# One operand turned on TensorE instead of through memory, in the tail of a two-layer graph network

## The chip, the core and the metric

The kernel runs on one core of a Trainium2 chip. The metric is the device time of one execution, in microseconds (us); lower is better. The core has TensorE (PE) for matrix products, VectorE (DVE), ScalarE (ACT) and GpSimd (POOL) for the rest, and SyncE (SP), which here only issues DMAs. Each engine takes its own instructions in order.

## What is computed

128 graphs go through the same two layers, each with 128 nodes of 512 features (`x`, float32) and a 128x128 adjacency matrix (`adj`). Cut to what matters:

```python
# layer 0
h = relu(layernorm(x))
r = relu(hypergraph_conv(h, adj, W1, b1))        # 512 -> 1024 features
y = hypergraph_conv(layernorm(r), adj, W2, b2)   # 1024 -> 512 features
x = x + (y + h)
# layer 1
h = relu(layernorm(x))
agg = (adj @ h) / max(rowsum(adj), 1e-6)
x = x + relu(concat([h, agg]) @ W.T)             # W: 512 x 1024
# hypergraph_conv(h): D^-1 H B^-1 H^T (h @ W.T) + b, with H = (adj != 0)
```

## The kernel before, in words

The work of one graph is cut into some fifty small stages, each a function with the graph's number as its argument. Each stage issues its instructions at once, in the order in which the stages are called; there is no scheduler that moves them. The function `step(s)` calls the stages of several graphs in turn, so that while one graph is in its first weighted product another is in its last one. `head()` starts this pipeline up, and `tail()` runs it dry for the last five graphs, called a, b, c, d and e (e is graph 127). The order of every engine's instructions is therefore the order of these calls, written out by hand.

A weighted product (`product`, L387) keeps near-float32 precision with three parts of each operand: a high part (`h`), a low part (`l`) and a part for the difference (`d`). The bank whose name ends in `m` (`rm`, `gm`, `bm`, `am`) takes the products of high and low parts (L401), the bank ending in `d` (`rd`, `gd`, `bd`, `ad`) the third (L406). ScalarE then copies the main bank out and VectorE adds the difference bank. The names are: `r` for the first convolution, `g` for the second, `b` for layer 1's neighbour half ("mean"), and `a` for its own half ("self"), on which `aggregate` (L616) adds the mean's part through the adjacency (`anp`). `py` (L534) is the second convolution's product with the node matrix. The high part comes from ScalarE (L483), the low one from a subtraction on GpSimd or VectorE (`combine`, L80; GpSimd in pieces of 256 columns), the third from VectorE (L492).

TensorE contracts over the partitions, so an operand that lies with nodes on partitions has to be turned before a weighted product. Before the change every graph does it by a round trip: `trip_out` (L447) writes the tile to memory, four DMAs of `trip_in` (L455) read it back as 32x32 blocks in swapped places, and VectorE turns each block in place (L462). For layer 1 the stages are `layer1_norm` (L256: ScalarE, relu of the normalised `x_t`), `layer1_trip_out` (`h_scratch`), `layer1_trip_in` (`hb`), `layer1_turn` (`ht`), `layer1_high` (`hh`), `layer1_low` (`hl`) and `layer1_rest` (`hd`). The 1024-wide operand `n` and the adjacency (`an_scratch`, `anb`, L214) make such trips too. The read-back tile leaves its features in an order that goes with blocks of 32, and the weights are loaded in the same order.

`hb` of one graph and `gb_t`, the mean's result, share one buffer (tag "hbt"), so a graph's trip in waits until the graph before it has split its mean. Six banks of PSUM are handed round for products, two for small ones.

`fill(n)` (L94) issues matmuls of a constant over n columns into the next bank that is handed out, ahead of that bank's own product. They compute nothing that is used. They stand where TensorE would otherwise wait.

The order of the tail on TensorE is: `py` of c, first convolution of e, `b` and `a` of b, `g` of d, aggregate of b, filler, `py` of d, `b` and `a` of c, `g` of e, aggregate of c, filler, `py` of e, `b` and `a` of d, aggregate of d, filler, `b` and `a` of e, aggregate of e.

Of the kernel before, what the change touches and what calls it, by code (L numbers as in the profile page):

```python
# [7 lines left out]
FP = mybir.dt.float32  # L8
FR = mybir.dt.float32r
# [15 lines left out]
def gnn_kernel(  # L25
# [31 lines left out]
    nc = tc.nc  # L57
# [51 lines left out]
    def stage(f):  # L109

        def run(g, *a):
            key = f, g, *(v for v in a if type(v) is int)
            if 0 <= g < N and key not in done:
                done.add(key)
                f(g, *a)

        return run


# [104 lines left out]
    @stage  # L224
    def load_adj(g):
        ADJ[g] = pool.tile([P, P], FP, tag="adj", name="adj_t")
        nc.sync.dma_start(out=ADJ[g], in_=adj[g])
# [20 lines left out]
    @stage  # L248
    def scales(g, kind):
        t = STATS[kind, g]  # L250
        nc.vector.reciprocal(t[:, 4:5], t[:, 3:4])
        nc.vector.tensor_tensor(t[:, 5:6], t[:, 1:2], t[:, 4:5], MUL)  # L252
# [8 lines left out]
    @stage  # L261
    def mean_operator(g):

        a = ADJ.pop(g)
        deg = pool.tile([P, 1], FP, tag="deg", name="deg", bufs=2)
        nc.vector.tensor_reduce(deg, a, AX.X, ADD)
        nc.vector.tensor_scalar(deg, deg, EPS_DEG, 1.0 / 4096.0, MAX, MUL)
        nc.vector.reciprocal(deg, deg)
        nc.vector.tensor_scalar(a, a, deg, None, MUL)
        ADJ[g] = a  # L270

    @stage
    def mean_out(g):
        ANT[g] = trip_out(ADJ.pop(g), "an")

    @stage
    def mean_in(g):
        d = ANT[g]
        ANT[g] = pool.tile([P, P], FP, tag="anb", name="anb")
        load_blocks(ANT[g], d)  # L280
# [17 lines left out]
    @stage  # L298
    def mean_rest(g):
        SPLIT.pop(("an", g))()  # L300
# [112 lines left out]
    @stage  # L413
    def conv1_weights(g, half):
        PR[g, half] = product(Z[g], w1[half : half + 1], lambda pm: PY.update({(g, half): pm}), "r")

    @stage
    def conv1_main(g, half):
        if half == 0:
            R[g] = pool.tile([P, DH], FP, tag="r", name="r")  # L420
        copy(R[g][:, HALVES[half]], PY.pop((g, half)), AF.Copy, scale=DN[g][:, 1:2])  # L421

    @stage
    def conv1_out(g, half):
        r, dn = R[g][:, HALVES[half]], DN[g]
        nc.vector.scalar_tensor_tensor(r, PR.pop((g, half)), dn[:, 0:1], r, MUL, ADD)  # L426

    @stage
    def conv1_bias(g, half, eng=nc.gpsimd):
        r = R[g][:, HALVES[half]]  # L430
        combine(eng, r, r, b1_bc[:, HALVES[half]], ADD)
# [5 lines left out]
    @stage  # L437
    def inner_spread(g):
        spread((2, g), R[g], pool.tile([P, DH], mybir.dt.bfloat16, tag="junk", name="junk"), DH)
# [26 lines left out]
    @stage  # L466
    def inner_out(g):
        NT[g] = trip_out(R.pop(g), "n")

    @stage  # L470
    def inner_in(g):
        NT[g] = trip_in(NT[g], "t2", "n")
# [24 lines left out]
    @stage  # L497
    def inner_turn(g):
        NT[g] = turned(NT[g], "t1", "n")

    @stage
    def inner_high(g):
        NT[g] = split_high(("n", g), NT[g], ("t3", "t2", "t1"))

    @stage
    def inner_low(g, *eng):
        NT[g][0](*eng)

    @stage
    def inner_rest(g):  # L510
        N_LEFT[g] = NT.pop(g)[1]()


    @stage
# [12 lines left out]
    @stage  # L527
    def conv2_bias(g, eng=nc.gpsimd):
        combine(eng, G[g], G[g], c0, ADD)

    @stage
    def conv2_nodes(g):
        PY[g] = py = small_bank("py")
        nc.tensor.matmul(py, S.pop(g), G.pop(g), start=True, stop=True)  # L534
# [11 lines left out]
    @stage  # L546
    def layer1_spread(g):
        spread((3, g), X[g], H3[g], D)

    @stage  # L550
    def layer1_norm(g):
        normalise((3, g), H3[g], X[g], AF.Relu)

    @stage
    def layer1_trip_out(g):
        H3T[g] = trip_out(H3.pop(g), "h")
# [9 lines left out]
    @stage  # L566
    def layer1_high(g):
        H3T[g] = split_high(("h", g), H3T[g], ("h2", "h3", "h1"))

    @stage  # L570
    def layer1_low(g, *eng):
        H3T[g][0](*eng)

    @stage
    def layer1_rest(g):
        H_LEFT[g] = H3T.pop(g)[1]()

    @stage
    def layer1_mean(g):
        PB[g] = product(H_LEFT[g], w3[:1], lambda pm: PY.update({("b", g): pm}), "b")  # L580
# [14 lines left out]
    @stage  # L595
    def layer1_mean_low(g, *eng):
        GB[g][0](*eng)
# [21 lines left out]
    @stage  # L619
    def layer1_self_out(g):  # L620
        o, pd = OP[g]
        nc.vector.scalar_tensor_tensor(o, pd, 4096.0, o, MUL, ADD)
# [301 lines left out]
    def tail():  # L924
        a, b, c, d, e = range(N - 5, N)
        layer1_self_main(a)
        conv2_bias(c)
        layer1_high(b)
        conv2_nodes(c)
        layer1_self_out(a)  # L930
        mean_out(b)
        inner_out(d)
        inner_in(d)
        finish(a)
        layer1_low(b)
        load_adj(c)
        mean_in(b)
        conv1_main(e, 0)
        conv2_out(c)
        conv1_weights(e, 1)  # L940
        layer1_sums(c)
        layer1_spread(c)
        layer1_rest(b)
        conv1_out(e, 0)
        conv1_main(e, 1)
        layer1_mean(b)
        inner_turn(d)
        scales(c, 3)
        layer1_self(b)
        conv1_out(e, 1)  # L950
        inner_high(d)
        conv1_bias(e, 0)
        layer1_norm(c)
        layer1_mean_main(b)
        mean_transpose(b)
        conv1_bias(e, 1)
        inner_low(d)
        layer1_mean_out(b)
        layer1_trip_out(c)
        inner_sums(e)  # L960
        layer1_mean_high(b)
        inner_spread(e)
        scales(e, 2)
        inner_rest(d)
        layer1_mean_low(b)
        conv2_weights(d)
        mean_operator(c)
        mean_rest(b)
        layer1_mean_rest(b)
        aggregate(b)  # L970
        inner_norm(e)
        conv2_main(d)
        layer1_trip_in(c)
        conv2_weights_out(d)
        layer1_turn(c)
        layer1_self_main(b)
        conv2_bias(d)
        layer1_high(c)
        fill(384)
        conv2_nodes(d)  # L980
        layer1_self_out(b)
        mean_out(c)
        inner_out(e)
        load_adj(d)
        inner_in(e)
        finish(b)
        layer1_low(c)
        mean_in(c)
        conv2_out(d)
        layer1_sums(d)  # L990
        layer1_rest(c)
        layer1_spread(d)
        layer1_mean(c)
        inner_turn(e)
        scales(d, 3)
        layer1_self(c)
        inner_high(e)
        layer1_norm(d)
        layer1_mean_main(c)
        mean_transpose(c)  # L1000
        layer1_mean_out(c)
        inner_low(e)
        layer1_trip_out(d)
        layer1_mean_high(c)
        mean_operator(d)
        inner_rest(e)
        layer1_mean_low(c, nc.vector)
        conv2_weights(e)
        mean_rest(c)
        layer1_mean_rest(c)  # L1010
        aggregate(c)
        conv2_main(e)
        layer1_trip_in(d)
        conv2_weights_out(e)
        layer1_turn(d)
        layer1_self_main(c)
        conv2_bias(e)
        layer1_high(d)
        fill(768)
        conv2_nodes(e)  # L1020
        layer1_self_out(c)
        layer1_low(d)
        mean_out(d)
        finish(c)
        mean_in(d)
        conv2_out(e)
        load_adj(e)
        layer1_sums(e)
        layer1_rest(d)
        layer1_mean(d)  # L1030
        layer1_spread(e)
        scales(e, 3)
        layer1_self(d)
        layer1_norm(e)
        layer1_mean_main(d)
        mean_transpose(d)
        layer1_mean_out(d)
        layer1_trip_out(e)
        layer1_mean_high(d)
        mean_operator(e)  # L1040
        layer1_mean_low(d, nc.vector)
        mean_rest(d)
        layer1_mean_rest(d)
        aggregate(d)
        layer1_trip_in(e)
        layer1_turn(e)
        layer1_self_main(d)
        layer1_high(e)
        layer1_self_out(d)
        mean_out(e)  # L1050
        layer1_low(e, nc.vector)
        mean_in(e)
        layer1_rest(e)
        fill(1536)
        layer1_mean(e)
        finish(d)
        layer1_self(e)
        layer1_mean_main(e)
        mean_transpose(e)
        layer1_mean_out(e)  # L1060
        layer1_mean_high(e)
        mean_rest(e)
        layer1_mean_low(e)
        layer1_mean_rest(e)
        aggregate(e)
        layer1_self_main(e)
        layer1_self_out(e)
        finish(e)
# [40 lines left out]
```

## Time and profile before

| | us |
|---|---|
| median of 4 runs | 2503.28 |
| lowest and highest run | 2502.23 to 2504.00 |
| the profiled execution | 2503.60 |
| its span, first to last instruction | 2501.8 |
| TensorE busy | 2475.6 (99%) |
| VectorE, ScalarE, GpSimd busy | 1999.5, 1935.0, 1713.2 |
| span from 2441 on, roughly the tail | 61 |
| first matmul of e's product `bm` | 2489.50 |
| TensorE's last matmul ends | 2497.20 |

The profile is of one execution. Its times are counted from the first instruction. A timeline line gives start, duration, engine, source line, operation, output and inputs, and in brackets the idle time before it with what ended it. The chain of waits is followed back from the last instruction. A window line gives the busy time of the engines in a stretch in the order TensorE, its weight loads, VectorE, ScalarE, GpSimd, then the granted clock of TensorE, the DMA share and GB/s. Neighbouring instructions of one engine overlap a little, so that a VectorE operation of 0.69 us is followed by the next one 0.61 us after its start. The profiled execution spends 1.8 us outside its span.

### The profile page before, as it was taken

The numbers are of one execution on the slowest core, as the hardware profiler recorded it, in microseconds if no ns is written. First come the engines' busy times: TensorE is split into PE (matmuls) and PEld (weight loads), VectorE is DVE, ScalarE is ACT, GpSimd is POOL, SyncE is SP. The second block draws the span as 40 slices with busy tenths as digits, with TensorE's granted clock in tenths as the row PEclk, the third lists the DMA queues.
The fourth block names the chain that finished last, engine by engine and source line by source line (L and its number), as shares of the span: only waits on it lengthen the run. The fifth ranks groups of instructions, "written<-read, shape, count | busy, mean of one in ns | idle before, by whom it ended". The sixth has DMA issues, their size and how long they took to land.

```text
span 2501.8 us, 41081 instructions
## 1 busy us (share of the span) xinstructions
PE 2475.6 (99%) x11196; PEld 2004.0 (80%) x11196; DVE 1999.5 (80%) x4910; ACT 1935.0 (77%) x4112; POOL 1713.2 (68%) x2284
## 2 busy tenths in 40 slices
PE   8899999999999999999999999999999999999998
PEld 5688888888888888888888888888888888888886
DVE  7888887887888788888878888887887888788785
ACT  6788778778877877887787788778778877877874
POOL 2476677677667767766776776677677667767763
PEclk9999999999999999999999999999999999999999
DMA  6333443443344344334434433443443344344332
GB/s 176 108 120 119 131 126 120 128 131 120 118 126 132 120 128 131 120 119 131 127 120 128 131 120 118 131 128 120 128 129 122 119 132 126 120 128 130 120 113 94
DMA packets 409671, 311.87 MB, mean 125 GB/s; under 512 B 176736, under 2 KB 340576, under 8 KB 409440
## 3 DMA queue, kind: packets, MB, share of 16 engines
q1 hardware_dynamic: 408608, 309.18, 40.0%
q8 instruction: 88, 1.44, 0.3%
q14 instruction: 143, 1.17, 0.2%
q10 hardware_dynamic: 576, 0.07, 0.0%
q0 software_dynamic: 256, 0.01, 0.0%
HBM read 166.47 MB, written 142.61 MB: 124 GB/s over the span
## 4 chain that ended last, share of the span: by engine, by line
PE 95%; DVE 2%; DMA 1%; ACT 1%; SPq 1%; issue 0%; POOL 0%; POOLq 0%; DVEq 0%; ACTq 0%
PE rm L401 18%; PE gm L401 18%; PE gd L406 9%; PE bm L401 9%; PE am L401 9%; PE rd L406 9%; PE bd L406 5%; PE ad L406 4%; PE pz L359 4%; PE py L534 4%; PE am L616 2%; PE ad L616 1%; PE ps_s L321 1%; DMA w11r<-in_w1t_dram 0%; DMA nb<-n_scratch 0%
## 5 line engine op out<-in xcount | busy, mean ns | idle before, releaser
L80 POOL TENSOR_TENSOR g<-g,c 128x256 f32<-128x256 f32 x252 | 180.9, 739 | 648.2 <-DVE g L525 648.2
L80 POOL TENSOR_TENSOR r<-r,b_bc 128x256 f32<-128x256 f32 x500 | 359.7, 741 | 54.1 <-DVE r L426 44.5
L80 POOL TENSOR_TENSOR nl<-nt,nh 128x256 fp32r<-128x256 f32 x504 | 357.5, 737 | 4.2 <-ACT nh L483 4.2
L80 POOL TENSOR_TENSOR x_t<-x_t,b_bc 128x256 f32<-128x256 f32 x256 | 242.2, 965 | 15.2 <-DMA b_bc<-in_b_dram 15.2
L240 ACT ACTIVATE h<-x_t 128x512 f32<-128x512 f32 x256 | 160.0, 625 | 106.3 <-DVE x_t L538 104.0
L610 ACT ACTIVATE o<-am 128x512 f32<-128x512 f32 x128 | 76.6, 598 | 214.1 <-PE am L616 214.1
L80 POOL TENSOR_TENSOR hl<-ht,hh 128x256 fp32r<-128x256 f32 x252 | 235.3, 953 | 2.5 <-ACT hh L483 2.3
L80 POOL TENSOR_TENSOR x_t<-x_t,h 128x256 f32<-128x256 f32 x256 | 180.8, 725 | 42.1 <-ACT h L256 42.1
L256 ACT ACTIVATE h<-x_t,st 128x512 f32<-128x512 f32 x256 | 206.1, 805 | 1.9 <-DVE st L252 1.8
L426 DVE SCALAR_TENSOR_TENSOR r<-rd,dinv,r 128x512 f32<-128x512 f32 x256 | 190.6, 745 | 19.1 <-PE rd L406 18.4
L589 DVE TENSOR_TENSOR gb_t<-bd,gb_t 128x512 f32<-128x512 f32 x128 | 88.6, 692 | 141.8 <-ACT gb_t L585 139.4
L538 DVE SCALAR_TENSOR_TENSOR x_t<-py,dinv,x_t 128x512 f32<-128x512 f32 x128 | 96.1, 751 | 123.7 <-PE py L534 123.6
L80 POOL TENSOR_TENSOR bl<-gb_t,bh 128x256 fp32r<-128x256 f32 x252 | 180.5, 735 | 15.5 <-PE am L401 15.5
L245 ACT ACTIVATE h<-x_t,st 128x512 f32<-128x512 f32 x256 | 183.9, 718 | 4.3
L359 PEld LDWEIGHTS pz<-s,h 128*128 128x128 f32 x1024 | 133.5, 191 | 66.3 <-ACT s L323 46.4
L421 ACT ACTIVATE r<-rm,dinv 128x512 f32<-128x512 f32 x256 | 172.9, 676 | 1.7 <-PE rm L401 1.7
L525 DVE TENSOR_TENSOR g<-gd,g 128x512 f32<-128x512 f32 x128 | 88.5, 692 | 97.7 <-PE gd L406 92.4
L462 DVE STREAM_TRANSPOSE nt<-nb 128x1024 f32<-128x1024 f32 x128 | 157.4, 1230 | 2.0 <-DMA nb<-n_scratch 1.6
L256 ACT ACTIVATE r<-r,st 128x1024 f32<-128x1024 f32 x128 | 157.7, 1232 | 1.3 <-DVE st L252 1.3
L492 DVE SCALAR_TENSOR_TENSOR nd<-nh,nl 128x1024 fp32r<-128x1024 f32 x128 | 155.8, 1217 | 0.0
L627 DVE SCALAR_TENSOR_TENSOR o<-o,x_t 128x512 f32<-128x512 f32 x128 | 151.0, 1180 | 4.3
L401 PE MATMUL rm<-w11h,z 128*128 128x512 f32 x512 | 151.4, 417 | 0.0
(138 smaller groups left out, 7207.2 us busy)
## 6 DMA issues: line engine op xcount, KB each, us to landing
n_scratch<-r SPq DMA_DIRECT2D x128, 512.0 KB, 2.7
nb<-n_scratch SPq DMA_DIRECT2D x512, 128.0 KB, 2.8
x_t<-in_x_dram SPq DMA_DIRECT2D x128, 256.0 KB, 3.0
h_scratch<-h SPq DMA_DIRECT2D x128, 256.0 KB, 2.0
hb<-h_scratch SPq DMA_DIRECT2D x512, 64.0 KB, 2.0
out_dram<-o SPq DMA_DIRECT2D x128, 256.0 KB, 2.1
adj_t<-in_adj_dram SPq DMA_DIRECT2D x128, 64.0 KB, 1.9
an_scratch<-adj_t SPq DMA_DIRECT2D x128, 64.0 KB, 1.7
```

The source lines that it names most:

```text
L80: eng.tensor_tensor(dst[:, s], a[:, s], b[:, s], op)
L240: copy(junk, src, func, accum_out=t[:, 0:1])
L245: copy(junk, src, AF.Square, bias=t[:, 1:2], accum_out=t[:, 2:3])
L256: copy(dst, src, func, bias=t[:, 5:6], scale=t[:, 4:5])
L359: nc.tensor.matmul(z[:, k * P : (k + 1) * P], H0[g][:, k * P : (k + 1) * P], S[g], start=True, stop=True)
L401: nc.tensor.matmul(pm, left[i](k), right(i, k), start=(i == 0 and k == 0), stop=(i == 1 and k == kk - 1))
L406: nc.tensor.matmul(pd, left[2](k), right(2, k), start=(k == 0), stop=(k == kk - 1), skip_group_check=True)
L421: copy(R[g][:, HALVES[half]], PY.pop((g, half)), AF.Copy, scale=DN[g][:, 1:2])
L426: nc.vector.scalar_tensor_tensor(r, PR.pop((g, half)), dn[:, 0:1], r, MUL, ADD)
L462: nc.vector.transpose(nt.rearrange("p k (i b) -> p k i b", b=B), t.rearrange("p i k a -> p k i a"))
L492: nc.vector.scalar_tensor_tensor(t, h, 2.0**-12, low, MUL, SUB)
L627: nc.vector.scalar_tensor_tensor(o, o, 0.0, X.pop(g), MAX, ADD)
```

## The change

For the last graph (e) alone, layer 1's operand no longer goes through memory. `layer1_norm_now` is `layer1_norm` with its output columns written in the order of blocks, `layer1_now` has TensorE transpose the four 128x128 pieces with a unit matrix into one bank, has ScalarE take the high part and VectorE the low part straight from that bank, and marks the five stages of the trip as done. `turn_unit` makes the unit matrix on GpSimd (a memset and a select) at the start of the tail, in a buffer that the first layer has finished with. `run.f` only lets a stage be marked as done. In the tail several calls change places, nine additions or subtractions move from GpSimd to VectorE (`nc.vector`), and the fillers are 512, 640 and 1408 columns in place of 384, 768 and 1536. The sequence on TensorE is the same but for the four transposes, which stand between the aggregate of d and the last filler. `head()` and `step(s)` are not touched. From line 117 on, a line of the changed kernel is one further down, and from the stages of `conv2_weights` on 41 further (L401 becomes L402, L616 becomes L657).

```diff
@@ -114,6 +114,7 @@
                 done.add(key)
                 f(g, *a)
 
+        run.f = f
         return run
 
 
@@ -509,6 +510,46 @@
     @stage
     def inner_rest(g):
         N_LEFT[g] = NT.pop(g)[1]()
+
+
+    def turned_now(key, src, tags, stages):
+        done.update((v.f, key[1]) for v in stages)
+        k = src.shape[1] // P
+        h, l = (left.tile([P, k, P], FP, tag=tag, name=key[0] + m).bitcast(FR) for tag, m in zip(tags, "hl"))
+        for i in range(0, k, 4):
+            b = bank("pt")
+            for n in range(4):
+                nc.tensor.transpose(b[:, n * P : (n + 1) * P], src[:, (i + n) * P : (i + n + 1) * P], TURN[0])
+            t = b.rearrange("p (n c) -> p n c", n=4)
+            copy(h[:, i : i + 4], t, AF.Copy, scale=DOWN)
+            nc.vector.tensor_tensor(l[:, i : i + 4], t, h[:, i : i + 4], SUB)
+
+        def rest():
+            d = left.tile([P, k, P], FP, tag=tags[2], name=key[0] + "d").bitcast(FR)
+            nc.vector.scalar_tensor_tensor(d, h, 2.0**-12, l, MUL, SUB)
+            return [lambda n, v=v: v[:, n] for v in (h, l, d)]
+
+        return None, rest
+
+    TURN = []
+
+    def turn_unit():
+        t = pool.tile([P, P], FP, tag="ht", name="unit")
+        nc.gpsimd.memset(t, 0.0)
+        nc.gpsimd.affine_select(out=t, in_=t, compare_op=ALU.not_equal, fill=1.0, base=0,
+                                pattern=[[-1, P]], channel_multiplier=1)
+        TURN[:] = [t]
+
+    def layer1_norm_now(g):
+
+        done.add((layer1_norm.f, g))
+        t = STATS.pop((3, g))
+        copy(H3[g].rearrange("c (k j a) -> c j k a", j=Q, a=B), X[g].rearrange("c (j k a) -> c j k a", j=Q, a=B),
+             AF.Relu, bias=t[:, 5:6], scale=t[:, 4:5])
+
+    def layer1_now(g):
+        H3T[g] = turned_now(("h", g), H3.pop(g), ("h2", "h3", "h1"),
+                            (layer1_trip_out, layer1_trip_in, layer1_turn, layer1_high, layer1_low))
 
 
     @stage
@@ -924,143 +965,140 @@
     def tail():
         a, b, c, d, e = range(N - 5, N)
         layer1_self_main(a)
-        conv2_bias(c)
+        inner_out(d)
+        turn_unit()
         layer1_high(b)
+        conv2_bias(c, nc.vector)
         conv2_nodes(c)
+        mean_out(b)
+        inner_in(d)
         layer1_self_out(a)
-        mean_out(b)
-        inner_out(d)
-        inner_in(d)
+        layer1_low(b, nc.vector)
+        conv1_main(e, 0)
         finish(a)
-        layer1_low(b)
-        load_adj(c)
-        mean_in(b)
-        conv1_main(e, 0)
+        conv1_weights(e, 1)
         conv2_out(c)
-        conv1_weights(e, 1)
         layer1_sums(c)
         layer1_spread(c)
+        load_adj(c)
         layer1_rest(b)
+        inner_turn(d)
         conv1_out(e, 0)
         conv1_main(e, 1)
+        inner_high(d)
         layer1_mean(b)
-        inner_turn(d)
         scales(c, 3)
         layer1_self(b)
         conv1_out(e, 1)
-        inner_high(d)
-        conv1_bias(e, 0)
-        layer1_norm(c)
+        mean_in(b)
+        conv1_bias(e, 0, nc.vector)
         layer1_mean_main(b)
         mean_transpose(b)
-        conv1_bias(e, 1)
-        inner_low(d)
+        layer1_norm(c)
+        conv1_bias(e, 1, nc.vector)
+        inner_low(d, nc.vector)
         layer1_mean_out(b)
-        layer1_trip_out(c)
+        mean_operator(c)
         inner_sums(e)
         layer1_mean_high(b)
         inner_spread(e)
+        layer1_mean_low(b, nc.vector)
         scales(e, 2)
         inner_rest(d)
-        layer1_mean_low(b)
+        inner_norm(e)
         conv2_weights(d)
-        mean_operator(c)
         mean_rest(b)
+        layer1_trip_out(c)
         layer1_mean_rest(b)
+        conv2_main(d)
         aggregate(b)
-        inner_norm(e)
-        conv2_main(d)
         layer1_trip_in(c)
         conv2_weights_out(d)
+        layer1_self_main(b)
         layer1_turn(c)
-        layer1_self_main(b)
-        conv2_bias(d)
         layer1_high(c)
-        fill(384)
+        fill(512)
+        conv2_bias(d, nc.vector)
+        inner_out(e)
         conv2_nodes(d)
         layer1_self_out(b)
         mean_out(c)
-        inner_out(e)
+        inner_in(e)
+        mean_in(c)
+        layer1_low(c, nc.vector)
+        conv2_out(d)
         load_adj(d)
-        inner_in(e)
-        finish(b)
-        layer1_low(c)
-        mean_in(c)
-        conv2_out(d)
+        layer1_rest(c)
         layer1_sums(d)
-        layer1_rest(c)
         layer1_spread(d)
         layer1_mean(c)
         inner_turn(e)
+        finish(b)
         scales(d, 3)
+        inner_high(e)
         layer1_self(c)
-        inner_high(e)
         layer1_norm(d)
+        mean_transpose(c)
         layer1_mean_main(c)
-        mean_transpose(c)
+        layer1_trip_out(d)
         layer1_mean_out(c)
+        mean_operator(d)
+        layer1_mean_high(c)
         inner_low(e)
-        layer1_trip_out(d)
-        layer1_mean_high(c)
-        mean_operator(d)
         inner_rest(e)
+        mean_rest(c)
         layer1_mean_low(c, nc.vector)
         conv2_weights(e)
-        mean_rest(c)
         layer1_mean_rest(c)
+        conv2_main(e)
+        mean_out(d)
+        conv2_weights_out(e)
+        layer1_trip_in(d)
         aggregate(c)
-        conv2_main(e)
-        layer1_trip_in(d)
-        conv2_weights_out(e)
         layer1_turn(d)
         layer1_self_main(c)
+        layer1_high(d)
         conv2_bias(e)
-        layer1_high(d)
-        fill(768)
+        fill(640)
+        layer1_low(d)
         conv2_nodes(e)
         layer1_self_out(c)
-        layer1_low(d)
-        mean_out(d)
-        finish(c)
         mean_in(d)
         conv2_out(e)
+        layer1_rest(d)
         load_adj(e)
+        layer1_mean(d)
         layer1_sums(e)
-        layer1_rest(d)
-        layer1_mean(d)
+        finish(c)
         layer1_spread(e)
+        layer1_mean_main(d)
+        layer1_self(d)
         scales(e, 3)
-        layer1_self(d)
-        layer1_norm(e)
-        layer1_mean_main(d)
         mean_transpose(d)
         layer1_mean_out(d)
-        layer1_trip_out(e)
         layer1_mean_high(d)
-        mean_operator(e)
+        mean_rest(d)
+        layer1_norm_now(e)
         layer1_mean_low(d, nc.vector)
-        mean_rest(d)
         layer1_mean_rest(d)
         aggregate(d)
-        layer1_trip_in(e)
-        layer1_turn(e)
+        mean_operator(e)
         layer1_self_main(d)
-        layer1_high(e)
+        mean_out(e)
+        mean_in(e)
+        layer1_now(e)
         layer1_self_out(d)
-        mean_out(e)
-        layer1_low(e, nc.vector)
-        mean_in(e)
+        fill(1408)
         layer1_rest(e)
-        fill(1536)
         layer1_mean(e)
         finish(d)
+        layer1_mean_main(e)
+        layer1_mean_out(e)
+        mean_transpose(e)
         layer1_self(e)
-        layer1_mean_main(e)
-        mean_transpose(e)
-        layer1_mean_out(e)
+        mean_rest(e)
         layer1_mean_high(e)
-        mean_rest(e)
-        layer1_mean_low(e)
+        layer1_mean_low(e, nc.vector)
         layer1_mean_rest(e)
         aggregate(e)
         layer1_self_main(e)
```

## Prediction

> **What bounds the kernel now.** I read the page's busy shares first, then the windows of the last 62 us, the chain that ended last, and the timelines of TensorE and ScalarE. All times below are microseconds from the start of the span.
>
> ```profile
> PE 2475.6 (99%) x11196; PEld 2004.0 (80%) x11196; DVE 1999.5 (80%) x4910; ACT 1935.0 (77%) x4112; POOL 1713.2 (68%) x2284
> ```
>
> TensorE is full almost everywhere, so only stretches where it isn't can be worth anything. The windows (time, then PE, PEld, DVE, ACT, POOL busy) show where that is:
>
> ```profile
> 2440.00:2460.00 20.00, 20.00 (x87) 16.12 (x86) 12.26 (x25) 12.40 (x25) 10.34 (x14) 1.00 0.39 129
> 2460.00:2480.00 20.00, 18.69 (x70) 12.30 (x69) 13.51 (x25) 9.50 (x20) 9.20 (x12) 1.00 0.31 96
> 2480.00:2502.00 22.00, 14.79 (x52) 9.35 (x52) 10.39 (x24) 5.92 (x13) 1.42 (x2) 0.93 0.19 58
> ```
>
> The tail begins near 2441. From `py` of graph c (2444.54) TensorE still has 15.2 us of real work to d's `py`, 12.4 to e's, 7.0 to the end of d's aggregate and 6.1 for e: 40.7, so it could end at 2485.3. It ends at 2497.2: 11.9 us of stalls and filler. The largest are in the TensorE timeline; the bracket is idle time and its releaser:
>
> ```profile
> 2461.54 1.13 PE L534 MATMUL py<-g,s 128*128 128x512 f32 x2 [0.97 <-POOL g L80]
> 2476.10 1.13 PE L534 MATMUL py<-g,s 128*128 128x512 f32 x2 [0.33 <-POOL g L80]
> ...
> 2485.92 2.75 PE L94 MATMUL bm<-eps 128*128 128x512 f32 x6
> 2489.50 1.19 PE L401 MATMUL bm<-w30h,hh 128*128 128x512 f32 x4 [0.83 <-ACT hh L483]
> ```
>
> The filler of L94 only covers a wait: 2485.92 to 2489.50 is 3.58 us lost. The chain says what for:
>
> ```profile
> 2485.86 2.02 DMA hb<-h_scratch
> ...
> 2488.01 0.72 DVE ht L462
> ...
> 2488.81 0.64 ACT hh L483
> 2489.45 0.04 issue
> 2489.50 2.11 PE bm L401 x8
> ...
> 2494.50 0.74 POOL bl L80
> ```
>
> That is e's round trip. Its normalised operand is done at 2481.82 and `hh` at 2489.44: 7.6 us. It also does harm earlier, for ScalarE takes work in order:
>
> ```profile
> 2481.00 0.82 ACT L256 ACTIVATE h<-x_t,st 128x512 f32<-128x512 f32 x1 [0.43 <-DVE st L252]
> 2481.72 0.58 ACT L585 ACTIVATE gb_t<-bm 128x512 f32<-128x512 f32 x1
> ```
>
> Graph d's mean copy (L585) stands behind e's norm (L256), though its product was complete near 2480. The chain there names a DMA that had nothing to do with it.
>
> **What the Trainium skill says.** "TensorE: Matmul & The Clock Gate", PE-mode transpose: TensorE alone turns a full 128x128 at once, output goes to PSUM, about 275 ns each inside a kernel (bf16), and such instructions don't count as busy for the clock. Its Terms section calls the transpose mode four times faster for FP32. No run here shows a transpose yet; the trace's `pz` (L359), four plain fp32 products of the same shape, takes 0.89 in the chain. "DMA: Bandwidth & Descriptors", Anatomy of one DMA, gives a DMA some 2 us of fixed cost (measured there on GpSimd's path; here SP issues); the trace agrees (h_scratch 2.0, hb 2.0 to landing). "SBUF — State Buffer", Who interferes with whom: a VectorE instruction with two SBUF inputs contends with a GpSimd one that reads SBUF. The trace agrees: L627 takes 1.18 on average, 0.69 where POOL is idle.
>
> **The change part by part**, in the order of the tail. I pass durations of before along the new order of each engine, and take these costs: VectorE 512 columns 0.69 (the next starts 0.61 after), ScalarE 0.58 to 0.81, one weighted product 1.81 main and 0.91 difference.
>
> *Nine adds and subtractions from POOL to VectorE.* Twenty POOL instructions of 0.74 go (14.8). VectorE gets eight of 0.69 and one of 1024 columns, 1.22 as L492: 6.7. It idles 7.7 of 20 us in the first window and 6.5 in the second, and these are fitted in between waits, so I cost them at nothing; without that cover each delays what queues behind it by 0.6. For d's `py`: before, `g` leaves VectorE at 2459.99 and POOL ends at 2461.48; after, it is behind one block transpose (from 2460.59, 0.69), so 2461.28: `py` 0.2 earlier. fill(512) takes 0.86 as 768 columns take 1.29, and ends at 2460.6, hidden. For e's `py` the add stays on POOL: it moves by the same 0.2, to 2475.9, fill(640), 1.07, ending 0.7 before it.
>
> *SP's queue.* e's write and four block reads go. d's reads wait for c's mean parts, which come some 0.5 earlier since c's transposed adjacency is fetched sooner (VectorE idled 1.83 for it before). So `hh` of d no longer stops `bm` of d, and the POOL subtraction behind it ends earlier: d's `bd` starts at 2479.25 in place of 2479.82 and is complete at 2480.4. d's output now stands behind e's adjacency DMAs; nobody waits for it.
>
> *Norm of e behind d's mean copies.* e's `x_t` moves from 2477.66 to 2476.95 (one `finish` less ahead of it), its statistics end near 2479.9, then ScalarE does d's mean copy: 2479.9 to 2480.5. VectorE adds to 2481.2, ScalarE `bh` to 2481.9, VectorE `bl` to 2482.6 and `bd` to 2483.2 (e's degree work, 0.9 ahead of `bl` before, now follows). Aggregate's last matmul at 2483.25, before 2485.58: 2.3 gained. The norm itself lies in its shadow, done near 2482.7; with a permuted write I take its 0.81 of before. It may be dearer: it has 0.9 to spare.
>
> *Transposes and filler.* Four transposes follow the aggregate, from 2483.6 (0.34 behind its last matmul, as before). Cost: 0.22 (a quarter of `pz`) to 1.1 (four of 275 ns); I take 0.5. fill(1408) takes 1408/768 of 1.29, 2.35, and cannot start before them: to 2486.45. Beside it run `hh` (0.6, to 2484.8), `hl`, an output step and `hd` (to 2486.9; `bd` needs it 1.8 behind `bm`'s start). So `bm` starts at 2486.45, before 2489.50: 3.05. What is late next is the filler itself, not `hh`; some 1.6 us of the stall stay.
> The identity (memset and select on POOL) has no row in the trace: two POOL steps of 128 columns at the tail's start, from half of L80's 0.74 to ten times it; POOL's next work is some 25 us later, so I take nothing.
>
> *The end.* Before, VectorE takes `bd` 3.12 after `bm`'s start: 2489.57. Then `gb_t` 0.61, the adjacency transpose 0.31 (now behind it; its DMA lands near 2488.7), ScalarE's copy and `bh` to 2491.5, `bl` on VectorE to 2492.2 (POOL took 1.42), `bd` to 2492.8, aggregate to 2493.35. Before 2497.20: 3.85. What follows is unchanged.
>
> Sum: the profiled execution took 2503.6 (span 2501.8 and 1.8 around it), so 2499.75; the median of the four runs is 0.3 lower, so 2499.4. Since each wait I moved may take 0.1 more than I give it, I say 2499.5.
>
> **The rivals.**
> *Stalls vanish too.* TensorE's own floor after e's `py` would end d's aggregate 0.7 sooner; transposes at 0.22 give 0.3, fewer restarts 0.5 in all. That gives 2498.0. For it: all seven idle times that the timeline brackets in the tail end on waits that the change moves. Against: the filler is a hard wall of 2.35.
> *The permuted norm or e's adjacency is late.* At four times its price the norm takes 3.2, 2.4 more, of which 0.9 is covered: 1.5 lost, 2501.0. e's adjacency has 0.8 of slack (landing 2488.7, wanted 2489.5) and would have to take 2.3 more to do the same. The trace of before shows no permuted ScalarE write.
> *Slower: TensorE's clock falls to half in the tail.* The windows show 1.00 from 2440 to 2498, and 0.60 only over the last 3.8 us, behind TensorE's last matmul, which is what makes 0.93 of the last window above. The place is the stretch around the transposes, which the skill says aren't counted as busy, with filler cut by 128 columns twice. From there 7 us of matmuls remain, 14 at half speed; with a fall already at d's stalls (13 remaining) the loss is up to 13. It decides once over 3.85 us of matmul time is lost, so if the clock falls before about 2489. A fall at the transposes gives 2499.5 + 7 = 2506.5. Against it: the longest idle before is 0.97 us with no fall, and after it is shorter.
> That the change does not do what it says is excluded: no h_scratch DMA of e is left in the order.
>
> **How the numbers follow.** Forecast 0.72, stalls vanish 0.15, late norm or adjacency 0.08, half clock 0.05. The forecast's own range is 2498.6 to 2500.5 (transposes -0.3 to +0.6, 0.6 for the walk). The range 2498.0 to 2501.2 takes in half of the second and third. Faster by over 0.2% (about what a measurement of this kernel can tell from no change) means under 2498.3: the second case and the forecast's edge, 0.20. Slower by that means over 2508.3: most of the clock's case, 0.03. Within: 0.77.
>
> **What would show it.** `bm` of e near 2486.5, directly at the filler's end with no wait on `hh`; d's last aggregate matmul near 2483.3, ScalarE's L585 of d ahead of e's norm; `py` of d and e only 0.2 earlier; transposes near 0.5 in all; TensorE's last matmul near 2493.3; clock 1.00 until then. I am wrong if `bm` waits, if VectorE has a queue ahead of `bd` or `nd`, or if the first tail `py` already moves.

## The result, and the profile after

| | before | after |
|---|---|---|
| median | 2503.88 us (61 runs, 2501.76 to 2505.39) | 2500.57 us (41 runs, 2498.46 to 2502.27) |
| profiled execution / its span | 2503.6 / 2501.8 | 2501.4 / 2499.5 |
| `py` of graph c starts | 2444.54 | 2445.71 |
| from there to the end of TensorE's last matmul | 52.65 | 48.91 |

The ratio is 0.9987, 95% interval [0.9983, 0.9992]: 3.3 us less, within 0.2%. The forecast was 2499.5, its range 2498.0 to 2501.2.

The last row is the number to compare. I call it the *tail* below. The changed kernel's profile started its tail 1.17 us later than the one of before, although TensorE's instructions ahead of it are the same; the last section says what is known of that. In the tail itself 3.74 us went, where 3.85 was forecast. A place x in the profile of before is to be looked for at x + 1.17 in the profile of after.

The page's busy line of after: TensorE has four instructions more (the transposes), GpSimd is 14.9 us less busy (14.8 forecast) and VectorE 5.0 more. The forecast's 6.7 counted the nine operations alone; e's block transpose, 0.71, is gone as well.

```profile
PE 2476.1 (99%) x11200; PEld 2007.2 (80%) x11200; DVE 2004.5 (80%) x4918; ACT 1934.7 (77%) x4112; POOL 1698.3 (68%) x2266
```

The windows of after (time, then TensorE, weight loads, VectorE, ScalarE, GpSimd, granted clock):

```profile
2440.00:2460.00 20.00, 20.00 (x88) 16.15 (x87) 15.25 (x30) 12.82 (x24) 0.00 (x0) 1.00 0.40 132
2460.00:2480.00 20.00, 18.95 (x75) 13.41 (x74) 14.81 (x28) 9.23 (x20) 5.67 (x8) 1.00 0.31 90
2480.00:2496.00 16.00, 13.98 (x56) 9.89 (x56) 10.73 (x25) 6.24 (x13) 0.00 (x0) 1.00 0.13 41
```

The clock is 1.00 up to the end of the work. VectorE took the additions in the idle time it had: 15.25 of the first 20 us, where it was 12.26. GpSimd does nothing at all in the first and the last window.

The chain of after, from e's `py` to the last aggregate:

```profile
2476.83 1.12 PE py L575 x2
2477.95 1.91 PE bm L402 x8
2479.86 1.19 PE bd L407 x4
2481.05 1.82 PE am L402 x8
2482.88 0.93 PE ad L407 x4
2483.80 0.02 issue
2483.83 0.70 DVE bd L493
2484.53 0.04 issue
2484.57 0.50 PE ad L657
2485.07 0.44 PE pt L522 x4
2485.51 2.37 PE bm L94 x6
2487.88 1.81 PE bm L402 x8
...
2492.42 0.93 PE ad L407 x4
2493.34 0.02 issue
2493.37 0.70 DVE bd L493
2494.07 0.04 issue
2494.11 0.52 PE ad L657
```

The DMA, the block transpose and `hh` of e are gone from it. `bm` (L402) starts where the filler (L94) ends: the filler itself is now what e's product waits for. From d's `bm` on TensorE works without a gap but for the two places where VectorE's `bd` (L493) stands between a self product and the aggregate. TensorE takes the aggregate's first two matmuls beside it and is then idle for 0.32. In both places `bd` starts 0.03 behind the last matmul of the self product (L407), not behind an operand of its own.

ScalarE's timeline shows the order that was forecast: d's mean copy (L626) ahead of e's norm (L547, with permuted output), then `hh` straight from the transposes:

```profile
2480.82 0.58 ACT L626 ACTIVATE gb_t<-bm 128x512 f32<-128x512 f32 x1
...
2482.86 0.80 ACT L547 ACTIVATE h<-x_t,st 128x512 f32<-128x512 f32 x1
...
2485.60 0.60 ACT L524 ACTIVATE hh<-pt 128x512 fp32r<-128x512 f32 x1 [0.71 <-PE pt L522]
```

### The profile page after: what moved, and what is told of

It is laid out like the page before. It is cut to its first block, busy times and chain, and to the rows that moved or that the text cites. A ratio compares the mean times of both kernels' runs of the same rounds, so it can differ in the third digit from the quotient of the medians.

```text
span 2499.5 us, 41060 instructions
## 1 busy us (share of the span) xinstructions
PE 2476.1 (99%) x11200; PEld 2007.2 (80%) x11200; DVE 2004.5 (80%) x4918; ACT 1934.7 (77%) x4112; POOL 1698.3 (68%) x2266
## 3 DMA queue, kind: packets, MB, share of 16 engines
q14 instruction: 144, 1.17, 0.2%
## 4 chain that ended last, share of the span: by engine, by line
PE 96%; DVE 2%; ACT 1%; DMA 1%; issue 0%; POOL 0%; SPq 0%; DVEq 0%; POOLq 0%; ACTq 0%
PE rm L402 18%; PE gm L402 18%; PE gd L407 9%; PE bm L402 9%; PE am L402 9%; PE rd L407 9%; PE bd L407 5%; PE ad L407 5%; PE pz L360 4%; PE py L575 4%; PE am L657 2%; PE ad L657 1%; PE ps_s L322 1%; DMA w11r<-in_w1t_dram 0%; DMA w20r<-in_w2t_dram 0%
## 5 line engine op out<-in xcount | busy, mean ns | idle before, releaser
L493 DVE SCALAR_TENSOR_TENSOR nd<-nh,nl 128x1024 fp32r<-128x1024 f32 x128 | 155.8, 1218 | 0.0
L402 PE MATMUL rm<-w11h,z 128*128 128x512 f32 x512 | 151.4, 417 | 0.0
```

What stands on the lines that cost most here:

```text
L402: nc.tensor.matmul(pm, left[i](k), right(i, k), start=(i == 0 and k == 0), stop=(i == 1 and k == kk - 1))
L493: nc.vector.scalar_tensor_tensor(t, h, 2.0**-12, low, MUL, SUB)
```

## The experiments

My theory after reading both traces: the transposes cost little, the filler is the wall ahead of e's product, d's aggregate came earlier by the new order, and the two halves of the change need each other. The rivals: the order alone (with the additions on VectorE) earns it and turning is incidental; or the additions on VectorE earn it; or the filler is needed for the clock.

In the table all times are on the tail's own clock, from c's `py`: d's second product part `bd`, the last matmul of d's aggregate, the first of e's product `bm`, and from there to the last matmul's end. Each row is one profiled execution. The kernels that share the changed kernel's engines, buffers and (but for e's own calls) order up to d's aggregate agree there within 0.2 (38.85 to 39.02), so a difference of 0.1 between two rows says nothing.

| kernel | tail | `bd` of d | d's aggregate | `bm` of e | to the end |
|---|---|---|---|---|---|
| before | 52.65 | 35.28 | 41.04 | 44.96 | 7.70 |
| after | 48.91 | 34.15 | 38.86 | 41.72 | 7.19 |
| turning alone | 51.80 | 35.27 | 41.04 | 43.90 | 7.90 |
| order alone | 53.66 | 34.33 | 39.02 | 45.02 | 8.63 |
| order alone, long filler | 52.07 | 34.30 | 39.01 | 45.05 | 7.02 |
| adds on GpSimd | 50.73 | 35.22 | 39.93 | 42.79 | 7.94 |
| two bias adds on GpSimd | 49.90 | 35.10 | 39.84 | 42.70 | 7.21 |
| e's `bl` on GpSimd | 49.75 | 34.24 | 38.96 | 41.81 | 7.94 |
| turned twice | 49.35 | 34.15 | 38.85 | 42.14 | 7.21 |
| short filler | 47.67 | 34.17 | 38.88 | 40.55 | 7.12 |
| and adjacency earlier | 47.74 | 34.22 | 38.94 | 40.62 | 7.12 |
| and buffers of their own | 46.93 | 34.17 | 38.67 | 40.35 | 6.58 |

**Turning alone.** The order and engines of before, with e's trip replaced:

```diff
         layer1_self_main(a)
+        turn_unit()
...
-        layer1_norm(e)
+        layer1_norm_now(e)
...
-        layer1_trip_out(e)
...
-        layer1_trip_in(e)
-        layer1_turn(e)
...
         layer1_self_main(d)
-        layer1_high(e)
+        layer1_now(e)
...
-        layer1_low(e, nc.vector)
...
-        fill(1536)
+        fill(1408)
```

Expected: 

> The order of before and its engines, with e's transposes in place of the round trip and fill(1408). My theory (the order is what brings d's aggregate forward, the transposes only free e): d's aggregate stays where it was, 41.0 behind c's py; transposes 0.44 and filler 2.37 follow; bm near 44.2 against 44.96 before, and the end as before since POOL still makes bl: tail 51.9. Rival (the round trip by itself is the gain): tail near 49.5.

Measured: tail 51.80, 0.85 less than before; median 2503.88 against 2504.00, ratio 0.9999 [0.9991, 1.0007]. TensorE's timeline:

```profile
2486.47 0.51 PE L657 MATMUL ad<-bd,anp 128*128 128x512 f32 x1 [0.30 <-DVE bd L493]
2486.82 0.60 PE L522 MATMUL pt<-unit,h 128*128 128x128 f32 x4
2487.25 2.54 PE L94 MATMUL bm<-eps 128*128 128x512 f32 x6
...
2496.01 0.49 PE L657 MATMUL am<-bl,anp 128*128 128x512 f32 x1 [0.50 <-POOL bl L80]
```

The transposes stand right behind d's aggregate, and that is as late as before (41.04). The round trip is gone, but what runs beside it is not shorter. The filler is what e's product waits for here too: `hh` ends at 2488.10 and `bm` starts at 2489.33, a distance of 1.23 as in the changed kernel. So 0.85 is not all that turning alone could give; it was not run with a shorter filler.

**Order alone.** The changed kernel without the turning: e goes through memory again.

```diff
-        turn_unit()
...
-        layer1_norm_now(e)
+        layer1_norm(e)
+        layer1_trip_out(e)
...
         aggregate(d)
+        layer1_trip_in(e)
...
-        layer1_now(e)
+        layer1_turn(e)
+        layer1_high(e)
         layer1_self_out(d)
+        layer1_low(e, nc.vector)
```

Expected: 

> The order and engines of the changed kernel, but e's operand makes the round trip again, behind its later norm. My theory: d's aggregate comes at 38.9 as in the changed kernel, but the trip of 7.6 starts at 37.95, so hh ends at 45.6 and bm at 45.6 against 42.0: tail 52.5, about as before (52.66). Rival (the order alone is most of the gain): tail at or under 50.5.

Measured: d's aggregate is early (39.02), yet `bm` of e starts at 45.02, as before, and the tail is 53.66, 1.0 *longer* than before; median 2504.84, ratio 1.0003 [0.9995, 1.0012]. The timeline of TensorE and its windows show a clock at half speed, which I had not expected here; the tail is 1.2 above my figure:

```profile
2484.89 2.53 PE L94 MATMUL bm<-eps 128*128 128x512 f32 x6
2490.55 1.94 PE L402 MATMUL bm<-w30h,hh 128*128 128x512 f32 x4 [3.13 <-ACT hh L484]
```

```profile
2480.00:2490.50 10.50, 7.10 (x25) 4.39 (x25) 5.47 (x15) 4.06 (x9) 0.00 (x0) 1.00 0.25 83
2490.50:2494.20 3.70, 3.65 (x9) 2.89 (x10) 1.99 (x3) 0.00 (x0) 0.00 (x0) 0.54 0.27 84
2494.20:2499.00 4.80, 4.48 (x19) 3.25 (x18) 2.79 (x6) 2.03 (x4) 0.00 (x0) 1.00 0.00 0
```

The filler that was sized for the short path ends 3.13 us before `hh` comes, and e's product then runs at half clock for 3.41 us (from 2490.73 in the record of the granted clock, 0.18 behind the product's start).

**Order alone, long filler**, to test whether that idle time made the clock fall: `fill(3072)` in place of `fill(1408)`, and nothing else.

Expected: 

> The new order alone, with the trip through memory, with 3072 columns of filler ahead of e's product in place of 1408. The round trip still ends where it did, so the product should start at the same 45.0 us of the tail; only TensorE's 3.13 us without work shrink to about 0.4. Theory: it was the idle time that made the clock fall to half for 3.41 us in the tail, which cost about 1.2; then no half-clock stretch lies in the tail, the last matmul ends about 7.2 to 7.7 behind the product's start in place of 8.63, and the tail is about 52.5 in place of 53.66. Rival: the fall came by chance or from elsewhere; then it is there again and the tail stays near 53.7.

Measured: tail 52.07 (one run, 2503.17). `bm` starts at 45.05, within 0.03 of the same place, but its end comes 7.02 later in place of 8.63. TensorE's timeline and the window from there on:

```profile
2484.04 5.33 PE L94 MATMUL bm<-eps 128*128 128x512 f32 x12
2489.74 1.20 PE L402 MATMUL bm<-w30h,hh 128*128 128x512 f32 x4 [0.37 <-ACT hh L484]
```

```profile
2489.50:2496.50 7.00, 6.44 (x27) 4.99 (x27) 4.81 (x10) 2.14 (x5) 0.00 (x0) 1.00 0.14 45
```

So the fall cost 1.6 us, and with the idle time filled it did not come (one execution each). With the clock put aside, the order alone is worth 0.58 and turning alone 0.85; both together are worth 3.74. The two paths to e's product, d's aggregate on TensorE and e's operand, run beside each other: either alone leaves the other where it was. The 0.58 is all behind `bm` of e (7.02 against 7.70), where e's `bl` is now made by VectorE; `bm` itself starts no earlier.

**The adds.** All nine additions and subtractions that had moved to VectorE back on GpSimd; then two parts of that alone, which the diff shows.

```diff
-        conv1_bias(e, 0, nc.vector)
+        conv1_bias(e, 0)
...
-        conv1_bias(e, 1, nc.vector)
+        conv1_bias(e, 1)
...
-        layer1_mean_low(e, nc.vector)
+        layer1_mean_low(e)
```

Expected of all nine: 

> The changed kernel with all nine additions and subtractions back on POOL. My theory: only bl of e is on the path, 0.8, and 0.2 at d's py: tail 49.9. Rival (VectorE's fast halves bring the whole tail forward): tail over 51. Other rival (VectorE was overloaded by them): tail under 48.9.

Expected of the first two alone: 

> The changed kernel with the two bias additions of e's first convolution alone back on POOL. Theory from the run with all nine back: these two release e's statistics and its 1024-wide round trip, and so c's mean on ScalarE and d's block reads; d's aggregate comes 1.0 later, tail 49.9. Rival (another of the nine, or all together): tail 48.9 to 49.2.

Expected of the last one alone: 

> The changed kernel with e's low part of the mean alone back on POOL. My theory: 0.75 at the end, nothing earlier: tail 49.65. Rival: 48.9, if the adjacency's transpose sets the end instead.

Measured: 50.73 (+1.82; median 2501.97, ratio to before 0.9995 [0.9986, 1.0003]), 49.90 (+0.99) and 49.75 (+0.84), the last two from one run each. The 1.82 is 0.8 more than my theory of all nine allowed, which had only `bl` of e and 0.2 at d's `py`; the bias additions are what it missed. The two parts add up to 1.83, so the other six seem to be worth nothing in this order. VectorE's timeline with all nine on GpSimd, at the block transposes of e's 1024-wide operand and of d's layer 1 operand:

```profile
2465.33 1.25 DVE L463 STREAM_TRANSPOSE nt<-nb 128x1024 f32<-128x1024 f32 x1 [0.82 <-DMA nb<-n_scratch]
...
2476.32 0.71 DVE L463 STREAM_TRANSPOSE ht<-hb 128x512 f32<-128x512 f32 x1 [1.45 <-DMA hb<-h_scratch]
```

and in the changed kernel:

```profile
2465.11 1.25 DVE L463 STREAM_TRANSPOSE nt<-nb 128x1024 f32<-128x1024 f32 x1
...
2476.13 0.71 DVE L463 STREAM_TRANSPOSE ht<-hb 128x512 f32<-128x512 f32 x1 [0.84 <-DMA hb<-h_scratch]
```

These two profiles' tails start 0.82 apart (2444.89 and 2445.71), so on the tail's clock both are 1.0 later with GpSimd. With the two bias additions alone on GpSimd they are 0.98 and 0.95 later. That fits the order of the work: e's bias additions release its statistics, these the trip of its operand, and behind that lie c's mean and d's reads of `hb`.

**Turned twice**: the four transposes issued two times.

```diff
-            for n in range(4):
-                nc.tensor.transpose(...)
+            for _ in range(2):
+                for n in range(4):
+                    nc.tensor.transpose(...)
```

Expected: 

> Each of the four transposes is issued twice, with the same result. My theory (they lie on the path, filler and product queue behind them): tail 48.91 + 0.44 = 49.35. Rival (they hide beside VectorE's work): 48.9.

Measured: 49.35, so +0.44, and one run of 2500.82. The transposes lie on the path, with 0.11 each.

**Short filler**: `fill(384)` in place of `fill(1408)`.

Expected: 

> Measure: the tail, from the start of c's py on TensorE to the end of its last matmul; 52.66 us before, 48.90 after. My theory: e's product waits for the filler alone, since hh ends at 2486.20 and the filler near 2487.7. With 384 columns bm should start right behind hh, 1.45 earlier; then e's adjacency, which lands near 2490.1, takes back some 0.3 and hd 0.1: tail 47.9, median 1.0 lower than after. Rival (the filler holds the clock up): the clock of the last 10 us falls below 1.00 and the tail isn't shorter, or is longer.

Measured: tail 47.67, 1.24 less than after; median 2498.92 (16 runs) against 2504.00, ratio 0.9980 [0.9973, 0.9988]. No half-clock stretch in the tail. `bm` of e starts 1.17 earlier, not 1.45, and e's adjacency took nothing back: from there to the end it is 7.12, against 7.19.

```profile
2483.61 0.60 PE L522 MATMUL pt<-unit,h 128*128 128x128 f32 x4
2484.05 0.81 PE L94 MATMUL bm<-eps 128*128 128x384 f32 x2
2484.95 1.21 PE L402 MATMUL bm<-w30h,hh 128*128 128x512 f32 x4
```

`hh` of that kernel ends at 2484.90, and `bm` starts 0.05 behind it: now the operand is the last to come, so still less filler should gain nothing (not run).

**Adjacency earlier**, on top of the short filler: e's adjacency work moved ahead, so that less stands between e's `bm` and its mean parts. Each of the four calls is taken out where it stood; the diff shows the new places.

```diff
+        load_adj(e)
         layer1_trip_in(d)
...
+        mean_operator(e)
         layer1_turn(d)
...
         mean_in(d)
+        mean_out(e)
...
         layer1_rest(e)
+        mean_transpose(e)
```

Expected: 

> Short filler (384) and e's adjacency made ready earlier: its load ahead of d's block reads, its degree work in VectorE's gap before d's block transpose, its transposition behind hd of e. The only version with all of this. My theory: bm of e stays at 40.55 behind c's py, and the end behind it shortens from 7.12 to 6.95, the floor set by e's last product, since bl and bd no longer stand behind the adjacency's transpose: tail 47.5, median 5 under before. Rival (VectorE has no room for 0.9 before d's transpose): d's aggregate comes later than 38.9 and the tail is 48 or more.

Measured: 47.74, no gain (median 2500.05 against 2504.54, 0.9981 [0.9974, 0.9988]). That theory fell; VectorE's timeline at e shows what held the mean's parts instead:

```profile
2490.20 0.69 DVE L80 TENSOR_TENSOR bl<-gb_t,bh 128x512 fp32r<-128x512 f32 x1 [0.72 <-PE am L402]
2491.05 0.69 DVE L493 SCALAR_TENSOR_TENSOR bd<-bh,bl 128x512 fp32r<-128x512 f32 x1 [0.15 <-PE ad L407]
```

`bl` and `bd` read nothing that these matmuls make. They *write* into the buffers (tags "h3" and "h1") whose `hl` and `hd` the self product still reads. So does ScalarE's `bh` ahead of them, into the buffer of `hh` (tag "h2"): it started 0.15 behind its operand `gb_t`.

**Buffers of their own**, on top of that: d's and e's mean parts in the buffers of the 1024-wide operand, which are free by then.

```diff
-        GB[g] = split_high(("b", g), GB[g], ("h2", "h3", "h1"))
+        GB[g] = split_high(("b", g), GB[g], ("t3", "t2", "t1") if g >= N - 2 else ("h2", "h3", "h1"))
```

Expected: 

> The kernel with the short filler and e's adjacency work pulled ahead, and besides that the mean's three parts of graphs d and e in buffers of their own (those of the 1024-wide operand, which the tail has finished with) in place of the ones that layer 1's operand still holds. Theory: the mean's low part and its difference part wait for the self product to have read the operand's parts, 0.72 and 0.15 us at e and 0.15 at d, and these waits are what kept the earlier adjacency from showing. Without them e's low part starts 0.7 earlier and its difference part no longer waits for the product's last matmul: e's end comes 0.5 earlier and d's aggregate 0.2 earlier, tail from 47.74 to about 47.0, last matmul 6.6 behind the start of e's product in place of 7.12. Rival: the wait is a false attribution and the mean's own chain (product, addition, high part, low part) is as long; then the tail stays at 47.7.

Measured: tail 46.93, 0.81 less. The same two instructions:

```profile
2489.98 0.69 DVE L80 TENSOR_TENSOR bl<-gb_t,bh 128x512 fp32r<-128x512 f32 x1 [0.30 <-ACT bh L484]
2490.71 0.69 DVE L493 SCALAR_TENSOR_TENSOR bd<-bh,bl 128x512 fp32r<-128x512 f32 x1
```

The waits for TensorE are gone; `bl` waits for its own operand. Counted from `bm` of e it starts 0.42 earlier, not 0.7: of the 0.72 idle only 0.33 lay behind the end of its own operand `bh` (2489.87), and `bh` itself comes 0.11 earlier. d's aggregate comes 0.27 earlier and the end 0.54, where 0.2 and 0.5 were expected. The median is 2499.20 (21 runs) against 2504.02, ratio 0.9982 [0.9975, 0.9988]. This kernel has the shortest tail. The medians don't put the three versions with a short filler in an order, nor set them apart from the changed kernel: each was compared with before in its own set of runs, the intervals of the ratios overlap (here [0.9975, 0.9988], the changed kernel's [0.9983, 0.9992]), and what the start of an execution adds differs by more than 0.81 from run to run.

## Why the prediction was right

The mechanism and the sum held, one step had the wrong cause, and one wait was overlooked; these two errors nearly cancel. Step by step, with places of after less the 1.17:

- *Adds at nothing, `py` 0.2 earlier.* `py` of d at 2461.30 (forecast 2461.34), of e at 2475.66 (2475.9). Right for these places. But "I cost them at nothing" was wrong elsewhere: they carry a gain that I gave to another cause.
- *SP's queue.* I had d's `bd` 0.57 earlier and put it to c's transposed adjacency being fetched sooner. It came 1.13 earlier, and the experiment with the bias additions gives 0.95 of that to those two (34.15 against 35.10). The step failed in its cause and by half in its size. Three lines of the profile of before show that c's adjacency was not what held c's mean:

```profile
2468.03 0.57 ACT L585 ACTIVATE gb_t<-bm 128x512 f32<-128x512 f32 x1
...
2468.40 0.31 DVE L287 STREAM_TRANSPOSE ant<-anb 128x128 f32<-128x128 f32 x1 [1.83 <-DMA anb<-an_scratch]
2468.64 0.69 DVE L589 TENSOR_TENSOR gb_t<-bd,gb_t 128x512 f32<-128x512 f32 x1
```

  VectorE idled 1.83 for the adjacency, but its addition `gb_t` could not start before ScalarE's copy ended at 2468.60, and it started 0.04 behind that.
- *Norm of e behind d's mean copies.* Forecast for d's last aggregate matmul 2483.25, found 2483.40. The order on ScalarE is as forecast and the permuted write cost nothing (0.80, where the plain norm takes 0.80 to 0.82 in the tail of before). The agreement is largely luck: I had not seen that d's mean `bd` must wait for the self product to have read `hd`. In after, with GpSimd's bias additions and with GpSimd's `bl`, the aggregate comes 4.71, 4.74 and 4.72 behind the product's `bd`; with buffers of their own it is 4.50. From my own 2479.25 that wait gives 2483.96, 0.7 later than I said. The product part that came 0.56 earlier than forecast made up for most of it. From the product's `bd` to the aggregate it was 5.76 before; the forecast made it 4.00, and it is 4.71. No run takes apart what the norm's place, the mean copy and e's degree work each give of that 1.05.
- *Transposes 0.5.* 0.44 in the chain and 0.44 more when doubled. Neither figure behind my range was the right price. The upper one, 1.1, took the Trainium skill's figure ("TensorE: Matmul & The Clock Gate", PE-mode transpose, some 275 ns each for bf16 inside a kernel) as the price of each: one transpose is indeed recorded with 0.27 here, in float32, but the next starts 0.11 behind it. The lower one, 0.22, took a quarter of `pz` from that page's Terms section: the four transposes take half of what `pz`'s four products take. The lines show two records for each of those products (x8) and one for each transpose, all about 0.11 apart:

```profile
2426.56 1.05 PE L359 MATMUL pz<-s,h 128*128 128x128 f32 x8
...
2484.91 0.60 PE L522 MATMUL pt<-unit,h 128*128 128x128 f32 x4
```

  The page's note that transposes don't count as busy did no harm here: the clock stayed at 1.00 behind these four.
- *Filler the wall at 2.35, what is late next is the filler and not `hh`.* 2.37 in the chain, and the short filler proves it with 1.24.
- *Unit matrix at nothing.* Memset 0.20 and select 1.10, at 2438.1 to 2439.5 of after's own time; GpSimd's next work comes 28.12 later.
- *The end.* Forecast last matmul end 2493.35, found 2493.44. The overlooked wait is here too: e's `bd` stood 0.15 for the self product to have read `hd`.
- *The rival of the half clock* was possible, but not in this kernel: the longest idle time in its tail is 0.54, while the clock fell behind 3.13 in the order alone, which has no transposes. There it cost 1.6 and not 7, since the fall lasts 3.41 us. *Stalls vanish* did not come true: the filler stood in the way for 1.24, as said, and four idle times stayed (0.52, 0.54 and twice 0.32).
- *From the profile to the median.* The profiles' tails differ by 3.74, the medians by 3.3. That is inside the interval (2.0 to 4.3). The median of after, 2500.57, is in the stated range but just outside the 2498.6 to 2500.5 that I gave the forecast itself. Of the 1.07 above 2499.5, 0.60 is the base: the median of before was 2503.28 over four runs and is 2503.88 over 61.

## What to carry to other kernels

When two paths meet at one instruction, cost each with the other left as it was: here 0.85 and, with the clock put aside, 0.58 alone against 3.74 together. A filler that was sized for the wait that a change removes must be shortened with it, as far as the operand allows, and one sized for a short wait leaves TensorE idle when the long one comes back: here for 3.13 us, behind which the clock fell. If VectorE starts on a write just behind a matmul whose result it doesn't read, look at which buffer it writes.

## What the runs showed of the hardware

The clock fell in the tail after 3.13 us without a TensorE instruction, and for 3.41 us. "TensorE: Matmul & The Clock Gate", What's actually happening, describes such windows of 3413 ns that run freely, with half clock after an idle one; the recorded durations, 3412 to 3414, agree. In the order alone the changes of clock lie whole numbers of such windows apart (the clock was full for 2389.33 us before this fall, 700 of them). The window that ended as the clock fell thus began at 2487.32 and holds, by the records of the matmuls, 0.10 us of filler, the 3.13 idle and 0.18 of the product: an idle time a little under a window sufficed. With 0.37 us idle behind 5.3 us of filler it did not fall. This is one execution of each; where between these two the limit lies is not shown.

Half-clock stretches of the same 3.41 us begin also in the first 100 us of every profile here, in places and number that change: one in the profile of before (95.7), three in that of after (19.3, 80.7, 97.8). Graph by graph, the 1.17 us between these two profiles is there from graph 2 on and stays the same to the end. Over all ten experiments one to three such stretches go with tails that start between 2443.19 and 2445.52, but not in strict order. They are not the whole cause: the kernel with buffers of its own has the same three as after, at the same places within 0.01, and its tail starts 0.69 earlier. What makes the spread of a kernel's runs stays open; it is about as large as this change's gain, which is why I read the tails.
